# Layer 3's selective scan: the products du x B formed in PSUM by TensorE, tiles of two sequences by eight states, and every product with C on GpSimd

## The chip, the cores and the metric

The kernel runs on one core of a Trainium2 chip, in one launch. The metric is the device time of that core in microseconds (us), lower is better. The engines are called as the profile calls them: PE is TensorE (PEld its weight loads), DVE is VectorE, ACT is ScalarE, POOL is GpSimd, and SP is the engine whose queue issues the DMAs.

## The reference

The network has four layers in a row on an image batch of 8 x 64 x 64 x 64. Layers 0 to 2 (a spectral convolution and two state-space layers over whole images) are the same in both kernels. Layer 3 reads its input as one image of 64 channels by 128 by 128 and runs a bidirectional Mamba along one axis, and then another along the other. Cut to what matters, for one direction `i` of one axis:

```
xn = rms_norm(x, nw)
xc, z = split(xn @ ipw.T)                    # 256 channels each
xc = silu(causal_dwconv(xc, cw, cb))         # 4 taps
dt_, B, C = split(xc @ xpw.T)                # 4, 16 and 16 columns
dt = softplus(dt_ @ dtw.T + dtb)
h  = h * exp(dt[:, None] * A) + (dt * xc)[:, None] * B[None, :]     # a step of the scan, 256 x 16 states
y  = sum_n(h * C[None, :])
out = (y + D * xc) * silu(z) @ opw.T
```

The backward direction runs on the reversed sequence. Per axis the two outputs are joined, passed through a linear map and added to the input. The kernel takes sequences of 64 positions of its own layout; a scan must start anew at every sequence.

## The kernel before

`layer3` (from L1814) is a list of 256 steps: two axes `s`, sixteen chunks `c` of the image, four groups `g` of a chunk, and two directions `k`. A step holds eight sequences of 64 tokens, `W` = 512 tokens, for 256 channels. These lie as two halves `j` of 128 partitions beside each other, so that a tile is 128 x 1024 (`T` = 1024). `Step.prepare` makes a step's operands while the step before it is being scanned: the convolution as matmuls (L2004) and `u` by Silu (L2016), the projection (L2019), `dbl`, which is copied (L2022) and written to `bc` in HBM, `dt` (matmul L2028, Softplus at L415), `du` = dt x u (L2039, POOL), and `z` (L2042, L2052). At the first token of each sequence `dt` is set to 1e30 (L2056), so that the decay there is zero and one scan can run over all sequences.

`stream` (L433 on) runs over tiles, one for each of the 16 states `n` of each step, in an order written out by hand (`manual_schedule`). For each tile:

- `fetch` loads rows n of B and C, broadcast over the partitions, by one DMA (issued at L2060, 512 KB) into the pool `bc`;
- `multiply_b` (L484) forms hb = du x B on POOL, three tiles ahead;
- `decay` (L491) forms dA = exp(A dt) on ACT, in two halves;
- `scan` (L500) runs on DVE;
- `multiply_c` (L514) forms h x C, on POOL for the states in `Step.shared` (five of 16, or four in every fourth step) and on DVE for the others;
- `gather` sums the tile into `acc` in PSUM with the identity as weights (helper `mm`, L306: two matmuls of 128x512).

After 16 tiles `skip` (L2065) has added D x u, `drain` (L2069) multiplies acc with z, and after both directions `finish` makes the output (L2088, L2091, L2107). `begin` prepares the chunk to come: its input, the means of squares, their roots, and xn (L1967, POOL). The scratch tile `mm` in PSUM is one buffer that all preparation takes in turn. The tasks `begin` and `finish` advance by one piece at a time between tiles (`advance`).

Of the kernel before, what the change touches and what calls it, by code (L numbers as in the profile page):

```python
# [10 lines left out]
F32 = mybir.dt.float32  # L11
# [257 lines left out]
class Net:  # L269
# [1543 lines left out]

    def layer3(self, src, dst):  # L1814
# [8 lines left out]
        with ExitStack() as ctx:  # L1823
# [3 lines left out]
            pools = (pool("bc", 8), pool("hb", 4), pool("hc", 4), pool("h", 3), two(pool), pool("pa", 1, space=PSUM))  # L1827
            hp = pool("h3", 3, space=DRAM)

# [6 lines left out]
            class Weights:  # L1836
# [12 lines left out]
                def load(self):  # L1849
                    s = self.s  # L1850

                    spare = pools[0].tile([128, 2, W], F32, name="bc")
                    self.w_in = pools[0].tile([128, 2, W], F32, name="bc")
                    self.w_out = self.take("out", spare[:C, 0, :].rearrange("p (k t) -> p k t", k=2))
                    self.lin = spare[:C, 1, : 2 * C].rearrange("p (k t) -> p k t", k=2)
                    nc.sync.dma_start(self.lin, net.d["l3_lin"][:, s])
                    self.nw = self.take("nw")
                    self.take("in", self.w_in)


                    self.taps = [cp.tile([128, 2, 256], F32, name=f"taps{s}{k}") for k in range(2)]
                    for k in range(2):
                        for m in range(2):
                            for r in range(2):
                                row = net.d["l3_taps"][2 * s + k, m, r : r + 1, :]
                                nc.sync.dma_start(self.taps[k][r * C : r * C + C, m, :], row.to_broadcast([C, 256]))
                    self.cb, self.xp = self.take("cb"), self.take("xp")

                    both = cp.tile([128, 2, 256], F32, name=f"both{s}")
                    self.dtw, self.z = self.take("dtw", both[:4]), both[C:]  # L1870
                    self.dtb, self.A, self.D = self.take("dtb"), self.take("A"), self.take("D")

                def build(self):
                    s = self.s

                    ps = pools[5].tile([128, T], F32, name="acc")[:, : 4 * C]
# [41 lines left out]
            chunks = {}  # L1918

            def begin(s, c):  # L1920
# [35 lines left out]
                yield False  # L1956
                for r in range(2):
                    nc.sync.dma_start(
                        inv[r * C : r * C + C, :, ends[r]], row.rearrange("o (s t) -> o s t", t=HW).to_broadcast([C, 4 * H, HW])
                    )  # L1960
                yield False
                yield False
                yield False
                hold["xn"] = p2.tile([128, 4 * H, HW + 6], F32, name="xn")
                for g in range(4):
                    at = slice(g * H, g * H + H)
                    nc.gpsimd.tensor_tensor(hold["xn"][:, at], x[:, at], inv[:, at], ALU.mult)  # L1967

                    for _ in range(9 if g < 3 else 1):
                        yield False  # L1970
# [5 lines left out]
            class Step:  # L1976
                bc_shape, start, early, late = [128, 2, W], 1, 0, False
                first = staticmethod(lambda n: 0.0)
                keep = staticmethod(lambda n, h: None)
                shaped = staticmethod(lambda t: t.rearrange("p (j t) -> p j t", j=2))  # L1980
                spread = staticmethod(lambda t, m: t[:, m : m + 1, :].to_broadcast([128, 2, W]))

                def __init__(self, s, c, g, k):
                    self.s, self.c, self.g, self.k, self.rev = s, c, g, k, k == 1
                    self.w = weights[s]
                    self.shared = (2, 6, 10, 14) if k and g % 2 else (1, 4, 7, 10, 13)
                    self.lanes = [(slice(j * W, j * W + W), self.w.A[:, k, j, :]) for j in range(2)]
# [6 lines left out]
                def prepare(self):  # L1994
                    k, w, hold = self.k, self.w, chunks[self.s, self.c]
                    xn = hold["xn"][:, self.g * H : self.g * H + H, :]

                    def tokens(ps):
                        return ps.rearrange("p (s t) -> p s t", t=HW)

# [11 lines left out]
                    yield CALM  # L2012
                    u = self.u = p2.tile([128, T], F32, name="u")
                    for j in range(2):
                        at = slice(j * W, j * W + W)
                        nc.scalar.activation(u[:, at], px[:, at], AF.Silu, bias=w.cb[:, k, j : j + 1])  # L2016
                    pd = pp.tile([128, T], F32, name="mm")[:36, :W]
                    for j in range(2):
                        nc.tensor.matmul(pd, w.xp[:, k, j, :], u[:, j * W : j * W + W], start=j == 0, stop=j == 1)  # L2019
                    yield True  # L2020
                    dbl = p2.tile([36, W], F32, name="dbl")
                    nc.scalar.copy(dbl, pd)  # L2022
                    self.bc = hp.tile([NS, 2, W], F32, name="bc")
                    for m in range(2):
                        nc.sync.dma_start(self.bc[:, m, :], dbl[4 + m * NS : 4 + m * NS + NS])
                    pt = pp.tile([128, T], F32, name="mm")
                    for j in range(2):
                        nc.tensor.matmul(  # L2028
                            pt[:, j * W : j * W + W], w.dtw[:, k, j * 128 : j * 128 + 128], dbl[0:4], start=True, stop=True
                        )  # L2030
                    yield True
                    yield CALM
                    dt = self.dt = p2.tile([128, T], F32, name="dt")
# [4 lines left out]
                    du = self.du = p2.tile([128, T], F32, name="du")  # L2038
                    nc.gpsimd.tensor_tensor(du, dt, u, ALU.mult)  # L2039
                    pz = pp.tile([128, T], F32, name="mm")  # L2040
                    for j in range(2):
# [6 lines left out]
                        )  # L2048
                    yield True
                    yield CALM  # L2050
                    z = self.z = p2.tile([128, T], F32, name=f"z{k}")
                    nc.scalar.activation(z, pz, AF.Silu)  # L2052


                    at = HW - 1 if k else 0
                    nc.scalar.copy(dt.rearrange("p (s t) -> p s t", t=HW)[:, :, at], endless)  # L2056

                def load(self, n, t):
                    row = self.bc[n : n + 1].rearrange("o m t -> o (m t)")
                    nc.sync.dma_start(t.rearrange("p m t -> p (m t)"), row.to_broadcast([128, 2 * W]))  # L2060

                def skip(self, acc):
                    for j in range(2):
                        at = slice(j * W, j * W + W)
                        nc.tensor.matmul(acc[:, at], self.w.skip[self.k][:, j, :], self.u[:, at], start=True, stop=False)  # L2065
                    return True

                def drain(self, acc):
                    nc.vector.tensor_tensor(self.z, acc, self.z, ALU.mult)  # L2069
                    chunks[self.s, self.c][f"y{self.k}"] = self.z  # L2070

                def done(self):
# [4 lines left out]
                    if self.k == 0 and self.g == 0 and more < 4 * NB:  # L2077
# [34 lines left out]
            with tc.manual_schedule():  # L2112
# [10 lines left out]
                self.stream(pools, (6, 3, 6), steps, behind)  # L2123
# [26 lines left out]
```

## Time and profile before

| what | value |
| --- | --- |
| runs shown | 24,770.57, 24,780.73 and 24,781.64 us; median 24,780.73 |
| span of the profiled execution | 24,763.3 us, 17.4 us under that median (an own time of this execution is not given apart) |
| mean granted clock of TensorE | 0.940 |
| layer 3 in the span | from 11,517 us (first matmul of L2004) to the end, 13,246 us |
| a step of layer 3 (of 256) | 51.74 us |
| matmuls and weight loads in the span | 53,146 of each |

The page of a profile gives for each engine the busy time and its share of the span, then the span in 40 slices (each digit is the busy share in tenths, the row PEclk the granted clock). Groups of instructions are named by line, engine, operation and tiles, "out<-in", with shapes; after the bar come busy time and the mean duration of one in ns, and after the next bar the idle time of the engine before them with what ended it. A busy PE is not a PE at its peak: matmuls overlap, and their ends are modelled. A matmul of f32 operands appears in the trace as two MATMUL records with a weight load each.

### The profile page before, as it was taken

To read this page: it belongs to the slowest core of one execution; us is meant where nothing else is said; L and a number is where in the kernel's file an instruction comes from. 1 tells how busy PE (TensorE), PEld (TensorE's weight loads), DVE (VectorE), ACT (ScalarE), POOL (GpSimd) and SP (SyncE) were. 2 spreads that over 40 slices of the span, in tenths; PEclk is the share of its full clock that TensorE was granted. 3 is DMA by queue.
4 is the path that set the end of the run, shared out by engine and by line. 5 is a ranking of instruction groups with operands and counts; after the bars stand their busy time and mean duration, and the time that the engine had idled before them with its cause. 6 is when DMAs were issued, how large, how long until landed. Compare 5 with 4: busy or idle time off the path is not lost. (4 is left out here: it accounts for less than half of the span.)

```text
span 24763.3 us, 192937 instructions
## 1 busy us (share of the span) xinstructions
PE 21205.6 (86%) x53146; PEld 8272.3 (33%) x53146; DVE 22452.5 (91%) x12956; ACT 14796.2 (60%) x18824; POOL 22125.0 (89%) x10580
## 2 busy tenths in 40 slices
PE   8877888888888888888888888888888888888888
PEld 6522333333333323322333333333333333333333
DVE  5399999999999779978999999999999999999999
ACT  4355555555555456624666666666666666666666
POOL 0199999999999669977999999999999999999999
PEclk9888999999999999999999999999999999999999
DMA  2399899898998669933555555555555555555554
GB/s 65 93 319 326 308 321 318 310 319 314 313 318 311 238 211 339 343 103 93 168 173 169 173 167 173 168 173 167 173 169 173 168 173 169 173 169 173 169 173 158
DMA packets 1835292, 5282.68 MB, mean 213 GB/s; under 512 B 533712, under 2 KB 539924, under 8 KB 1831904
## 3 DMA queue, kind: packets, MB, share of 16 engines
q1 hardware_dynamic: 1809632, 5207.00, 63.0%
q10 hardware_dynamic: 24576, 63.33, 0.7%
q8 instruction: 423, 6.93, 0.1%
q14 instruction: 661, 5.41, 0.1%
HBM read 5112.85 MB, written 156.11 MB: 213 GB/s over the span
## 5 line engine op out<-in xcount | busy, mean ns | idle before, releaser
L484 POOL TENSOR_TENSOR hb<-du,bc 128x1024 f32<-128x1024 f32 x4608 | 10746.4, 2360 | 204.5 <-DVE h L500 137.9
L306 PE MATMUL acc<-hc,ident 128*128 128x512 f32 x18560 | 8788.0, 614 | 87.6 <-DVE img L1266 49.9
L491 ACT ACTIVATE dA<-dt,w_A 128x512 f32<-128x512 f32 x8192 | 5673.1, 693 | 3923.3 <-DVE hc L514 2873.1
L500 DVE TENSOR_TENSOR_SCAN dA<-dA,hb 128x1024 f32<-128x1024 f32 x3320 | 7580.9, 2283 | 188.4 <-ACT dA L491 101.0
L306 PE MATMUL acc<-h,ident 128*128 128x512 f32 x8064 | 4652.9, 706 | 2430.0 <-POOL h L514 2400.9
L306 PEld LDWEIGHTS acc<-hc,ident 128*128 128x128 f32 x18560 | 3639.8, 200 | 5214.2 <-issue 4562.5
L484 POOL TENSOR_TENSOR hb<-du,b 128x1024 f32<-128x1024 f32 x2048 | 4919.7, 2476 | 467.4 <-DVE dA L500 205.6
L514 DVE TENSOR_TENSOR hc<-dA,bc 128x1024 f32<-128x1024 f32 x3232 | 3956.8, 1224 | 244.4 <-issue 4.5
L491 ACT ACTIVATE dA<-dt,w_l_A 128x1024 f32<-128x1024 f32 x2560 | 2863.6, 1119 | 1004.6 <-DVE hc L514 764.6
L500 DVE TENSOR_TENSOR_SCAN h<-dA,hb 128x1024 f32<-128x1024 f32 x1416 | 3229.1, 2280 | 82.0 <-ACT dA L491 80.2
L306 PEld LDWEIGHTS acc<-h,ident 128*128 128x128 f32 x8064 | 1569.1, 212 | 5155.8 <-POOL h L514 3484.1
L514 POOL TENSOR_TENSOR h<-h,bc 128x1024 f32<-128x1024 f32 x1376 | 3243.1, 2357 | 8.3 <-DVE h L500 8.3
L500 DVE TENSOR_TENSOR_SCAN dA<-dA,carry,hb 128x1024 f32<-128x1024 f32 x1320 | 3094.2, 2344 | 124.9 <-POOL hb L484 57.2
L514 DVE TENSOR_TENSOR hc<-dA,c 128x1024 f32<-128x1024 f32 x1408 | 1723.7, 1224 | 118.3 <-DMA c<-bc 7.2
L514 POOL TENSOR_TENSOR h<-h,c 128x1024 f32<-128x1024 f32 x640 | 1566.4, 2447 | 7.5 <-ACT carry L1249 6.9
L491 ACT ACT_TABLE_LOAD x1128 | 1447.2, 1283 | 19.7
L500 DVE TENSOR_TENSOR_SCAN h<-dA,carry,hb 128x1024 f32<-128x1024 f32 x600 | 1404.6, 2341 | 36.4 <-ACT dA L491 25.2
L1249 ACT COPY carry<-dA 128x1 f32<-128x1 f32 x1056 | 169.4, 160 | 1654.3 <-DVE hc L514 1613.4
L2004 PE MATMUL mm<-xn,taps 128*128 128x512 f32 x2048 | 932.9, 597 | 1.1 <-ACT z L2052 1.1
L721 POOL MEMSET xf<- 128x24 f32 x33 | 4.3, 141 | 851.4 <-PE ps L742 725.2
L2019 PE MATMUL mm<-u,w_xp 128*36 128x512 f32 x1024 | 489.8, 601 | 143.0 <-ACT u L2016 136.3
L2039 POOL TENSOR_TENSOR du<-dt,u 128x1024 f32<-128x1024 f32 x256 | 603.0, 2355 | 9.9 <-ACT dt L415 9.9
(320 smaller groups left out, 18494.0 us busy)
## 6 DMA issues: line engine op xcount, KB each, us to landing
bc<-bc SPq DMA_DIRECT2D x4096, 512.0 KB
b<-bc SPq DMA_DIRECT2D x2048, 512.0 KB
c<-bc SPq DMA_DIRECT2D x2048, 512.0 KB
bc<-bc SPq DMA_DIRECT2D x512, 1024.0 KB
tmp<-rs SPq DMA_DIRECT2D x93, 512.0 KB
raw<-x SPq DMA_DIRECT2D x64, 512.0 KB
inv<-rs SPq DMA_DIRECT2D x64, 512.0 KB
tmp<-x SPq DMA_DIRECT2D x192, 128.0 KB
```

The source lines that it names most:

```text
L306: self.nc.tensor.matmul(o, lhsT, r, start=start, stop=stop)
L484: nc.gpsimd.tensor_tensor(s.shaped(hb[i]), s.shaped(s.du), B.pop(i), ALU.mult)
L491: nc.scalar.activation(dA[i][:, cut], s.dt[:, cut], AF.Exp, scale=A[:, n : n + 1])
L500: nc.vector.tensor_tensor_scan(h[:, way], dA[i][:, way], hb.pop(i)[:, way], s.first(n), ALU.mult, ALU.add)
L514: engine.tensor_tensor(s.shaped(o), s.shaped(h), CC.pop(i), ALU.mult)
L721: nc.gpsimd.memset(x[:, :, HW:], 0.0)
L1249: nc.scalar.copy(self.carry[:, n : n + 1], h[:, last : last + 1])
L2004: nc.tensor.matmul(tokens(px[:, j * W : j * W + W]), w.taps[k][:, m, j * 128 : j * 128 + 128], xn[:, :, f : f + HW], start=m == 0, stop=m ...
L2019: nc.tensor.matmul(pd, w.xp[:, k, j, :], u[:, j * W : j * W + W], start=j == 0, stop=j == 1)
L2039: nc.gpsimd.tensor_tensor(du, dt, u, ALU.mult)
```

## The change

Layer 3 runs a new function, `octets`, instead of `stream`. Layers 0 to 2 keep theirs.

A tile is still 128 x 1024 and there are still 16 for each step, but it now holds one half `j` of the channels, two sequences, eight states (half `q` of the 16) and 64 tokens. Four tiles (index `i` = 0 to 3, the eight sequences in pairs) make a group with one 128 x 4096 buffer `dA`; a step has four groups, (q, j) = (0,0), (0,1), (1,0), (1,1).

- *du x B.* In `prepare`, `du` is transposed by eight matmuls with the identity as moving operand and copied to `duT`, tokens on partitions; B is made a second time with tokens on partitions (eight matmuls with 16 columns) and copied to `BT`. `build` multiplies BT with a mask, so that `D` holds B on diagonals of 32 x 32 blocks, for eight states beside each other (DVE, 128x1024, twice a step). `spread` then makes a tile of hb directly in PSUM by four matmuls, each with 32 rows of duT as weights and 256 columns of D. Tokens lie in halves of 32 (`h`); `e` is the sequence of the pair. hb has two buffers of two banks, sequence e in bank e.
- *Scan* (DVE) reads dA and hb from PSUM, and writes in place over dA.
- *Products with C* (`multiply`) are all on POOL, in place. The row of C is loaded for one (q, i) and used for both j: eight DMAs of 512 KB for a step; B is no longer broadcast by DMA.
- *gather* sums a group, when its four tiles are multiplied, by eight matmuls of 128x512 with the identity, four in each of two iterations.
- xn is formed for one step of two (k = 0) in `prepare` instead of ahead for a whole chunk, and `begin` waits with its broadcast of `inv` until the chunk before has formed all its xn.

In every iteration t the order of issue is: the DMA for t+4, the product with C of tile t-1, the matmuls of hb for t+1, the exps of the next group (3, 3, 2 and 0 of the eight), the sums (where t mod 4 is 1 or 2), the scan of t, the drain, and a piece of preparation.

The diff, cut to its core:

```diff
+    def octets(self, pools, steps, behind):
...
+        def where(t):
+            s, r = divmod(t, per)
+            q, j = first.supers[r // 4]
+            return steps[s], q, j, r % 4
...
+        def fetch(t):
+            if t < total:
+                s, q, j, i = where(t)
+                if j == 0:
+                    need(t, "bc")
+                    tile_ = cp_.tile([128, T], F32, name="c")
+                    nc.sync.dma_start(tile_, s.row(q, i).to_broadcast([128, T]))
+                    for e in range(first.lanes):
+                        CC[t + 4 * e] = tile_
+        def decay(g, ns):
+            if 4 * g < total:
+                need(4 * g, "dt")
+                s, q, j, _ = where(4 * g)
+                if ns[0] == 0:
+                    sup[g] = sp.tile([128, 8, 8, 64], F32, name="dA")
+                for n in ns:
+                    o = sup[g][:, :, n, :].rearrange("p s (h t) -> p s h t", h=2)
+                    nc.scalar.activation(o, s.times(j), AF.Exp, scale=s.rates(j)[:, 8 * q + n : 8 * q + n + 1])
+        def spread(t):
+            if t < total:
+                need(t, "duT")
+                s, q, j, i = where(t)
+                o = hb[t] = hbp[t % 2].tile([128, 2, 8, 64], F32, name="hb")
+                Q, g0 = divmod(2 * i, 4)
+                for h in range(2):
+                    for e in range(2):
+                        at = slice(32 * (g0 + e), 32 * (g0 + e) + 32)
+                        nc.tensor.matmul(
+                            o[:, e, :, 32 * h : 32 * h + 32],
+                            s.duT[at, j, 2 * h + Q, :],
+                            s.D[q][at, 2 * h + Q].rearrange("p n t -> p (n t)"),
+                            start=True,
+                            stop=True,
+                        )
+        def part(t):
+            i = t % 4
+            return sup[t // 4][:, 2 * i : 2 * i + 2].rearrange("p s n t -> p (s n t)")
+        def scan(t):
+            s = steps[t // per]
+            way = slice(None, None, -1) if s.rev else slice(None)
+            h, x = part(t), hb.pop(t).rearrange("p s n t -> p (s n t)")
+            nc.vector.tensor_tensor_scan(h[:, way], h[:, way], x[:, way], 0.0, ALU.mult, ALU.add)
+        def multiply(t):
+            nc.gpsimd.tensor_tensor(part(t), part(t), CC.pop(t), ALU.mult)
+        def gather(g, ns):
+            s, q, j, _ = where(4 * g)
+            if ns[0] == 0 and q == 0:
+                acc[j] = pa.tile([128, 512], F32, name="acc")
+                s.skip(j, acc[j])
+            o = acc[j].rearrange("p (s t) -> p s t", t=64)
+            for n in ns:
+                nc.tensor.matmul(o, self.ident, sup[g][:, :, n, :], start=False, stop=q == 1 and n == 7)
+            if ns[-1] == 7:
+                sup.pop(g)
+        work, self.held, self.urgent = Task(steps[0].prepare()), None, deque()
+        work.run()
+        for q in range(2):
+            steps[0].build(q)
+        for t in range(4):
+            fetch(t)
+        decay(0, range(8))
+        spread(0)
+        work = None
+        for t in range(total + 4):
+            at, r = divmod(t, per)
+            more = at + 1 < len(steps)
+            if r == 0 and more:
+                steps[at + 1].ready()
+                while self.held or self.urgent:
+                    self.advance(behind)
+                work = Task(steps[at + 1].prepare())
+            fetch(t + 4)
+            if 0 < t <= total:
+                multiply(t - 1)
+            if r == 2 and 0 < at < len(steps):
+                steps[at].build(1)
+            if r == per - 5 and more:
+                need(t + 5, "duT")
+                steps[at + 1].build(0)
+            spread(t + 1)
+            ns = (range(3), range(3, 6), range(6, 8), ())[t % 4]
+            if ns:
+                decay(t // 4 + 1, ns)
+            if t >= 5 and t % 4 in (1, 2):
+                g = (t - 5) // 4
+                if 4 * g < total:
+                    gather(g, range(4) if t % 4 == 1 else range(4, 8))
+            if t < total:
+                scan(t)
+            if t >= 7 and t % 4 == 3:
+                s, q, j, _ = where(t - 7)
+                if q == 1:
+                    s.drain(j, acc.pop(j))
+                    if j == first.lanes - 1:
+                        s.done()
+            if work is not None and not (self.held and work.said is None):
+                work.step()
+                if work.over:
+                    work = None
+            self.advance(behind, work is None or work.said is not True)
+        while behind or self.urgent or self.held:
+            self.advance(behind)
...
-            pools = (pool("bc", 8), pool("hb", 4), pool("hc", 4), pool("h", 3), two(pool), pool("pa", 1, space=PSUM))
+            hbp = [pool(f"hb{j}", 1, space=PSUM) for j in range(2)]
+            pools = (pool("dA", 3), pool("cc", 6), pool("D", 2), hbp, pool("pa", 2, space=PSUM))
             hp = pool("h3", 3, space=DRAM)
+            mask = cp.tile([128, 32], F32, name="mask")
+            nc.vector.tensor_tensor(mask, self.ident[:, :32], self.ident[:, 32:64], ALU.add)
+            for r in range(2, 4):
+                nc.vector.tensor_tensor(mask, mask, self.ident[:, 32 * r : 32 * r + 32], ALU.add)
...
+                while c and used.get((s, c - 1), 0) < 4 or s and not c and used.get((0, 2 * NB - 1), 0) < 4:
+                    yield False
...
-                yield False
-                yield False
-                hold["xn"] = p2.tile([128, 4 * H, HW + 6], F32, name="xn")
-                for g in range(4):
-                    at = slice(g * H, g * H + H)
-                    nc.gpsimd.tensor_tensor(hold["xn"][:, at], x[:, at], inv[:, at], ALU.mult)
-                    for _ in range(9 if g < 3 else 1):
-                        yield False
...
+                lanes, supers = 2, [(0, 0), (0, 1), (1, 0), (1, 1)]
                     self.s, self.c, self.g, self.k, self.rev = s, c, g, k, k == 1
-                    self.w = weights[s]
-                    self.shared = (2, 6, 10, 14) if k and g % 2 else (1, 4, 7, 10, 13)
-                    self.lanes = [(slice(j * W, j * W + W), self.w.A[:, k, j, :]) for j in range(2)]
+                    self.w, self.D = weights[s], {}
...
-                    xn = hold["xn"][:, self.g * H : self.g * H + H, :]
+                    at = slice(self.g * H, self.g * H + H)
+                    if k == 0:
+                        xn = hold["xn"] = p2.tile([128, H, HW + 6], F32, name="xn")
+                        nc.gpsimd.tensor_tensor(xn, hold["x"][:, at], inv[:, at], ALU.mult)
+                        used[self.s, self.c] = self.g + 1
+                        yield
+                    xn = hold["xn"]
...
-                        nc.scalar.activation(u[:, at], px[:, at], AF.Silu, bias=w.cb[:, k, j : j + 1])
-                    pd = pp.tile([128, T], F32, name="mm")[:36, :W]
+                        o, x = halves(u[:, at]), px[:, at].rearrange("p (s h t) -> p s h t", h=2, t=32)
+                        nc.scalar.activation(o, x, AF.Silu, bias=w.cb[:, k, j : j + 1])
+                    yield
+                    pd = pp.tile([128, T], F32, name="mm")
                     for j in range(2):
-                        nc.tensor.matmul(pd, w.xp[:, k, j, :], u[:, j * W : j * W + W], start=j == 0, stop=j == 1)
-                    yield True
-                    dbl = p2.tile([36, W], F32, name="dbl")
-                    nc.scalar.copy(dbl, pd)
-                    self.bc = hp.tile([NS, 2, W], F32, name="bc")
-                    for m in range(2):
-                        nc.sync.dma_start(self.bc[:, m, :], dbl[4 + m * NS : 4 + m * NS + NS])
+                        o = pd[:36, :W].rearrange("p (s h t) -> p s h t", h=2, t=32)
+                        nc.tensor.matmul(o, w.xp[:, k, j, :], halves(u[:, j * W : j * W + W]), start=j == 0, stop=j == 1)
+                    for m in range(4):
+                        for j in range(2):
+                            nc.tensor.matmul(
+                                pd[:, W + m * NS : W + m * NS + NS], chunk(u, j, m), w.xp[:, k, j, 4 : 4 + NS], start=j == 0, stop=j == 1
+                            )
+                    yield True
+                    dbl = p1.tile([36, W], F32, name="dbl")
+                    nc.scalar.copy(dbl, pd[:36, :W])
+                    BT = self.BT = p2.tile([128, 4, NS], F32, name="BT")
+                    nc.scalar.copy(BT.rearrange("p m n -> p (m n)"), pd[:, W : W + 4 * NS])
+                    bc = hp.tile([2, 8, 8, HW], F32, name="bc")
+                    for q in range(2):
+                        at = 4 + NS + 8 * q
+                        nc.sync.dma_start(bc[q].rearrange("s n t -> n s t"), dbl[at : at + 8].rearrange("n (s t) -> n s t", t=HW))
+                    self.bc = bc
+                    yield
                     pt = pp.tile([128, T], F32, name="mm")
                     for j in range(2):
-                        nc.tensor.matmul(
-                            pt[:, j * W : j * W + W], w.dtw[:, k, j * 128 : j * 128 + 128], dbl[0:4], start=True, stop=True
-                        )
-                    yield True
-                    yield CALM
-                    dt = self.dt = p2.tile([128, T], F32, name="dt")
+                        o = pt[:, j * W : j * W + W].rearrange("p (h s t) -> p h s t", h=2, t=32)
+                        x = dbl[0:4].rearrange("p (s h t) -> p h s t", h=2, t=32)
+                        nc.tensor.matmul(o, w.dtw[:, k, j * 128 : j * 128 + 128], x, start=True, stop=True)
+                    yield True
...
-                    du = self.du = p2.tile([128, T], F32, name="du")
-                    nc.gpsimd.tensor_tensor(du, dt, u, ALU.mult)
...
+                    du = p1.tile([128, T], F32, name="du")
+                    nc.gpsimd.tensor_tensor(du, dt, u, ALU.mult)
+                    yield True
                     z = self.z = p2.tile([128, T], F32, name=f"z{k}")
                     nc.scalar.activation(z, pz, AF.Silu)
-                    at = HW - 1 if k else 0
-                    nc.scalar.copy(dt.rearrange("p (s t) -> p s t", t=HW)[:, :, at], endless)
-                def load(self, n, t):
-                    row = self.bc[n : n + 1].rearrange("o m t -> o (m t)")
-                    nc.sync.dma_start(t.rearrange("p m t -> p (m t)"), row.to_broadcast([128, 2 * W]))
-                def skip(self, acc):
+                    at = (1, 31) if k else (0, 0)
                     for j in range(2):
-                        at = slice(j * W, j * W + W)
-                        nc.tensor.matmul(acc[:, at], self.w.skip[self.k][:, j, :], self.u[:, at], start=True, stop=False)
-                    return True
-                def drain(self, acc):
-                    nc.vector.tensor_tensor(self.z, acc, self.z, ALU.mult)
+                        o = dt[:, j * W : j * W + W].rearrange("p (h s t) -> p h s t", h=2, t=32)[:, at[0], :, at[1]]
+                        nc.scalar.copy(o, endless[:, :8])
+                    self.dt = dt
+                    yield
+                    pu = pp.tile([128, T], F32, name="mm")
+                    for j in range(2):
+                        for m in range(4):
+                            at = (j * 4 + m) * 128
+                            nc.tensor.matmul(pu[:, at : at + 128], chunk(du, j, m), net.ident, start=True, stop=True)
+                    yield True
+                    duT = p2.tile([128, 2, 4, 128], F32, name="duT")
+                    nc.scalar.copy(duT.rearrange("p j m d -> p (j m d)"), pu)
+                    self.duT = duT
+                def build(self, q):
+                    o = self.D[q] = pools[2].tile([128, 4, 8, 32], F32, name="D")
+                    nc.vector.tensor_tensor(
+                        o,
+                        mask.unsqueeze(1).unsqueeze(1).to_broadcast([128, 4, 8, 32]),
+                        self.BT[:, :, 8 * q : 8 * q + 8].unsqueeze(3).to_broadcast([128, 4, 8, 32]),
+                        ALU.mult,
+                    )
+                def times(self, j):
+                    return self.dt[:, j * W : j * W + W].rearrange("p (h s t) -> p s h t", h=2, t=32)
+                def rates(self, j):
+                    return self.w.A[:, self.k, j, :]
+                def row(self, q, i):
+                    return self.bc[q].rearrange("s n t -> (s n t)").unsqueeze(0)[:, i * T : i * T + T]
+                def skip(self, j, acc):
+                    u = self.u[:, j * W : j * W + W].rearrange("p (h s t) -> p s h t", h=2, t=32)
+                    acc = acc.rearrange("p (s h t) -> p s h t", h=2, t=32)
+                    nc.tensor.matmul(acc, self.w.skip[self.k][:, j, :], u, start=True, stop=False)
+                def drain(self, j, acc):
+                    z = self.z[:, j * W : j * W + W]
+                    nc.vector.tensor_tensor(z, acc, z, ALU.mult)
                     chunks[self.s, self.c][f"y{self.k}"] = self.z
...
-                    if self.k == 0 and self.g == 0 and more < 4 * NB:
+                    if self.k == 0 and self.g == 1 and more < 4 * NB:
...
-                self.stream(pools, (6, 3, 6), steps, behind)
+                self.octets(pools, steps, behind)
```

## The prediction

> **What bounds the kernel now.** I read the shares and slices of the page first, then busy time by stretch, then the groups of layer 3, then the timeline. Layer 3 runs from its first convolution matmul (L2004) at 11,517 us to the end of the span: 13,246 us for 256 steps, **51.74 us a step**. On the page:
>
> ```profile
> PE 21205.6 (86%) x53146; PEld 8272.3 (33%) x53146; DVE 22452.5 (91%) x12956; ACT 14796.2 (60%) x18824; POOL 22125.0 (89%) x10580
> PE   8877888888888888888888888888888888888888
> DVE  5399999999999779978999999999999999999999
> POOL 0199999999999669977999999999999999999999
> PEclk9888999999999999999999999999999999999999
> ```
>
> Layers 0 to 2 are not touched, so only the right half matters. There DVE and POOL are full, and PE is less full, though by little. A stretch inside layer 3 puts figures on it:
>
> ```profile
> core 0: us, PE busy (x) PEld busy (x) DVE busy (x) ACT busy (x) POOL busy (x), PEclk, DMA share, GB/s
> 16000.00:20000.00 4000.00, 3468.72 (x7287) 1319.14 (x7288) 3881.15 (x2199) 2722.73 (x3587) 3946.67 (x1724) 0.95 0.53 171
> ```
>
> POOL is busy 98.7% (51.1 us a step), DVE 97.0% (50.2), PE 86.7% (44.9), ACT 68.1% (35.2). POOL and DVE bound the stage together. The groups of layer 3 (12,000 to 24,000 us) give the prices:
>
> ```profile
> L484 POOL TENSOR_TENSOR hb<-du,bc 128x1024 f32<-128x1024 f32 x3720 | 8673.1, 2360 | 153.7 <-DVE h L500 118.3 <-DVE dA L500 34.9
> L500 DVE TENSOR_TENSOR_SCAN dA<-dA,hb 128x1024 f32<-128x1024 f32 x2616 | 5972.1, 2283 | 13.7 <-ACT dA L491 8.4 <-POOL hb L484 5.0
> L306 PE MATMUL acc<-hc,ident 128*128 128x512 f32 x10462 | 4912.4, 613 | 0.0
> L514 DVE TENSOR_TENSOR hc<-dA,bc 128x1024 f32<-128x1024 f32 x2615 | 3201.6, 1224 | 198.5 <-issue 4.0 <-PE acc L306 0.9 <-PE mm L2019 0.4
> L514 POOL TENSOR_TENSOR h<-h,bc 128x1024 f32<-128x1024 f32 x1105 | 2604.6, 2357 | 0.0
> ```
>
> The reader is to see that a product with B or C costs 2.36 us on POOL and 1.22 us on DVE, and a scan 2.28 us. The matmul's 613 ns is no price: matmuls overlap. The timeline has it:
>
> ```profile
> 20035.49 1.98 PE L306 MATMUL acc<-h,ident 128*128 128x512 f32 x4 [0.59 <-POOL h L514]
> 20037.40 1.98 PE L2042 MATMUL mm<-xn,both 64*128 64x512 f32 x4
> 20039.32 3.70 PE L306 MATMUL acc<-hc,ident 128*128 128x512 f32 x8
> ```
>
> Each f32 matmul is recorded as two passes; at full clock a 512-column pass starts every 0.429 us, so a 128x512 matmul holds PE for **0.86 us**. Between 20037.40 and 20039.32 lie 1.92 us for four passes (1.72): going to another shape of the array (64 rows here) costs **0.20 us**, of which 0.09 is the change and 0.10 a first weight load that nothing hides.
>
> [...] the 4-row matmuls of L2028 also start 0.429 us apart. [...] Layer 0 shows such pairs, 48 rows in each of two row groups:
>
> ```profile
> 639.72 2.00 PE L692 MATMUL pw<-w_l_phi,w_l_theta 48*128 48x256 f32 x16 [0.46 <-DVE W L299]
> ```
>
> Sixteen passes of 256 columns in 2.00 us, the last 0.16 of it pipeline tail: eight slots of 0.216 plus 0.10 at the start. Alone they would need 16 x 0.214 = 3.4. So two-way overlap is real, each matmul with weights of its own. [...] A scan from PSUM is not in the trace; the nearest row, z<-acc (L2069), takes 1.21 us from PSUM beside 1.22 for the SBUF product.
>
> **The change, part by part, per step.**
> *POOL.* Sixteen products du x B go (16 x 2.36 = -37.8). All products with C come to POOL: 16 x 2.36 instead of 4.75 on average. With du (2.36) and half of an xn (1.40) it has 37.8 + 2.4 + 0.7 = **40.8 us**.
> *DVE.* Loses 11.25 products (x 1.224 = -13.8), gains two builds of the diagonal blocks (128x1024, 2 x 1.22). Scans 36.5 + builds 2.4 + drains 1.3 = **40.3**.
> *ACT.* The exps keep number and size. Added: a copy of BT and one of duT (1.03, as z<-mm). About **37**.
> *DMA.* Eight rows of C of 512 KB instead of sixteen of B and C: the queue's load halves. It bounds nothing now (share 0.53), and the rows are asked for four tiles ahead, over 12 us, so I count no gain and no loss.
> *PE* gets what POOL loses:
> - sums into acc, 32 matmuls as before: 64 x 0.429 = 27.5
> - preparation as before: passes of 512 columns for taps 8, xp 4, dtw 4, z 4, skip 4, the output 5 (ten every second step), the mean 1: 30 x 0.429 = 12.9. (27.5 + 12.9 = 40.4 is today's sum; with the clock at 0.95 and tails it shows as 44.9.)
> - du x B: each tile has four matmuls of 32 rows and 256 columns, eight passes. Neighbours in the order lie in different row groups [...], so I take pairs: 4 slots x 0.216 = 0.86; 16 tiles: **13.8**. Bounds: 6.9 if four ran at once (but the third and fourth use the same row groups as the first two), 27.6 if none overlap.
> - eight small matmuls for BT and eight transposes of du, 32 passes. The nearest row, pt<-x of layer 0 with 128 columns, starts a pass every 0.11 us: 3.4.
> - changes of shape: per four tiles one burst, half a sum, a burst, half a sum, two bursts: four changes x 0.20, sixteen a step, and about nine around preparation and output: 5.0.
>
> Sum **62.6 us**, beside 40.8 on POOL: PE becomes the bound.
>
> *The new wait.* hb has two buffers, and the burst for tile t+1 waits for scan t-1; everything in PE's queue, the sum after it included, waits behind. Per four tiles by these durations: burst 0 to 1.0, half sum to 4.6, burst to 5.7, half sum to 9.2, two bursts to 11.3. The scan of the third burst runs from 10.5 to 12.8, and the next burst waits for it: 1.6 us idle in every 12.9. Preparation that falls there hides it (about two and a half of four times), leaving about **2.4 us**. What sat before scans and sums until now (hb from POOL, h from POOL, hc from DVE) goes, because these engines have over 20 us of slack.
>
> So 62.6 + 2.4 = **65.0 us a step**: (65.0 - 51.74) x 256 = +3,395 us. Added to the profiled span of 24,763.3 that is 28,158; the median of the runs is 17.4 us above the span, so **28,175 us**.
>
> **The rivals.**
> 1. *Pairs don't overlap with 32 rows* (shown only for 48 and 64). Burst 1.73: +13.8 a step, 78.8, so 31,700. Against it: layer 0 overlaps at the same 256 columns with weights loaded for each. 8%.
> 2. *The scan from PSUM is dearer.* It decides from about 3.8 us (16 x 3.8 + 3.8 = 64.6 on DVE); doubled to 4.56 it gives 16 x 4.56 + 3.8 = 77, about 31,200. Against it: z<-acc. Were it quicker than 2.28, only the 2.4 us of wait could go. 5%.
> 3. *The clock.* It stands at 0.95 [...]; but if thin bursts counted as idle, each tenth of PE's time at half clock adds 6.3 us a step, 1,600 us: 29,800. 4%.
> 4. *Other side: faster.* If the bursts ran nearly free beside other matmuls, POOL at 40.8 would set the pace, about 44 with its waits: (44 - 51.74) x 256 = -1,980, so 22,800. It decides only where PE falls below 51.7, that is where a burst costs under 0.2 us instead of 1.0 with its part of waits and changes. Even four at once (0.43) leaves 65.0 - 6.9 = 58. Against it: the sums fill all 128 rows. 2%, and 1% for no change.
>
> The order is written out by hand, so no scheduler can leave a product elsewhere; that the change doesn't do what it says I don't count.
>
> **How the numbers follow.** PE-bound with pairs has 80%. Its own ends: 61.1 us (wait filled, part of the changes hidden) gives 27,150; 71.3 (each wait for a scan open, PE held by ACT in preparation) gives 29,800, which takes in the mild case of the clock. The range 27,150 to 29,800 leaves out the rest. A measurement tells about 0.2%, 50 us, from no change; all main cases lie far beyond: slower 97%, same 1%, faster 2%.
>
> **What would show it.** Right: in layer 3 PE near 95% or more and PEclk near 1.0, DVE and POOL near 63%; PE idle mostly before L1869 and released by DVE scans; eight L1869 passes in about 1.0 us; shares of L1897 as those of L306 now. Wrong: eight passes in 1.7 us or more (rival 1), scans over 3 us (rival 2), PEclk under 0.9 (rival 3), or POOL near full with PE waiting for it.

## The result and the profile after

The changed kernel takes **28,495.5 us** (28,483.8 to 28,510.1), the kernel before 24,775.7 on the same chip: ratio **1.150, 95% interval 1.149 to 1.152**. The forecast was 28,175 us, in a range of 27,150 to 29,800. Layer 3 starts at 11,516 us as before (11,517) and ends the span at 28,488.7: 16,973 us, **66.3 us a step** instead of 51.74. The forecast was 65.0.

Shares and slices of the page, after:

```profile
PE 25730.0 (90%) x94106; PEld 11526.8 (40%) x94106; DVE 19878.4 (70%) x10847; ACT 14667.3 (51%) x19623; POOL 19925.3 (70%) x9364
PE   8778888888888889899999999999999999999999
DVE  5499999999986997566666666666666656666655
POOL 0399999999984996566666666666666666666666
PEclk9889999999999999899999999999999999999999
```

In the right part DVE and POOL have gone from 9 to 6, and PE from 8 to 9. The stretch inside layer 3, after (busy time of each engine, then granted clock, DMA share, GB/s):

```profile
16000.00:20000.00 4000.00, 3774.27 (x15350) 1796.40 (x15349) 2420.59 (x1217) 2101.36 (x2991) 2559.55 (x1059) 0.94 0.23 69
```

PE is busy 94.4%, DVE 60.5%, POOL 64.0%, and the DMA share has fallen from 0.53 to 0.23; it bounded nothing before, so that gains nothing. The groups of layer 3, after (12,000 to 28,000 us):

```profile
L1888 POOL TENSOR_TENSOR dA<-dA,c 128x1024 f32<-128x1024 f32 x3871 | 9525.4, 2473 | 5575.5 <-DVE dA L1885 5560.1
L1885 DVE TENSOR_TENSOR_SCAN dA<-dA,hb 128x1024 f32<-128x1024 f32 x3871 | 8724.1, 2278 | 5669.8 <-PE hb L1869 5117.6 <-PE mm L2184 494.3 <-POOL dA L1888 57.9
L1897 PE MATMUL acc<-dA,ident 128*128 128x512 f32 x15485 | 7662.6, 641 | 0.0
L1869 PE MATMUL hb<-D,duT 32*128 32x256 f32 x30968 | 3628.0, 411 | 817.2 <-DVE dA L1885 817.2
```

Read the idle columns as a chain: POOL waits for the scan, the scan waits for hb from PE, and PE alone waits little (817 us, for scans that free an hb buffer). The scan from PSUM costs 2.278 us, no more than the one from SBUF (2.283). The timeline of one stretch, after, PE's lines alone:

```profile
20003.06 1.13 PE L1869 MATMUL hb<-D,duT 32*128 32x256 f32 x8
...
20007.76 1.16 PE L1869 MATMUL hb<-D,duT 32*128 32x256 f32 x16
...
20058.01 1.16 PE L1869 MATMUL hb<-D,duT 32*128 32x256 f32 x16
...
20061.63 1.13 PE L1869 MATMUL hb<-D,duT 32*128 32x256 f32 x8 [2.46 <-DVE dA L1885]
...
20062.69 5.40 PE L1897 MATMUL acc<-dA,ident 128*128 128x512 f32 x8
```

Three things are in it. A burst (the four matmuls, eight passes, that make one tile of hb) takes 1.06 us to the next start when it stands alone, as forecast. **Two bursts on end (x16) that start together take no longer than one** (1.16 us against 1.13): four row groups at once. And after the wait of 2.46 us the eight passes of the sum take 5.40 us instead of 3.70, because part of them runs at half clock.

From the same trace, for each step: PE idle 3.7 us (5.6% of 66.3), of which 3.4 are waits for scans; by the clock's own record 7.4 us at half clock (between 12,000 and 24,000 us in 182 stretches of 3.41 us, 67 of 6.83 and 23 of 10.24), with PE busy in 7.2 of them, where it does half the work (a pass of 512 columns starts every 0.85 us there instead of 0.43): 3.6 us lost; what is left, 66.3 - 3.7 - 3.6 = **59.0 us, is PE's work at full clock**. All experiments below are read by this sum of three terms.

### The profile page after: what moved, and what is told of

It is laid out like the page before. It is cut to its first block, busy times and chain, and to the rows that moved or that the text cites. A ratio compares the mean times of both kernels' runs of the same rounds, so it can differ in the third digit from the quotient of the medians.

```text
span 28488.7 us, 260989 instructions
## 1 busy us (share of the span) xinstructions
PE 25730.0 (90%) x94106; PEld 11526.8 (40%) x94106; DVE 19878.4 (70%) x10847; ACT 14667.3 (51%) x19623; POOL 19925.3 (70%) x9364
## 4 chain that ended last, share of the span: by engine, by line
PE 58%; DVE 3%; ACT 1%; issue 0%; POOL 0%; DMA 0%; SPq 0%; POOLq 0%; ACTq 0%; DVEq 0%
PE acc L1897 28%; PE hb L1869 12%; PE mm L2146 3%; DVE dA L1885 3%; PE acc L2242 2%; PE mm L2268 2%; PE mm L2166 2%; PE mm L2163 2%; PE mm L2215 2%; PE mm L2193 2%; PE mm L2184 1%; PE pc L376 1%; PE mm L306 1%; PE ps L376 1%; PE mm L2265 0%
## 5 line engine op out<-in xcount | busy, mean ns | idle before, releaser
L1888 POOL TENSOR_TENSOR dA<-dA,c 128x1024 f32<-128x1024 f32 x4096 | 10076.6, 2472 | 5914.8 <-DVE dA L1885 5898.6
L1885 DVE TENSOR_TENSOR_SCAN dA<-dA,hb 128x1024 f32<-128x1024 f32 x4096 | 9230.8, 2278 | 6012.2 <-PE hb L1869 5415.4
L1897 PE MATMUL acc<-dA,ident 128*128 128x512 f32 x16384 | 8115.2, 641 | 1.2 <-POOL dA L1888 1.2
L1897 PEld LDWEIGHTS acc<-dA,ident 128*128 128x128 f32 x16384 | 3217.6, 204 | 4249.5 <-issue 4247.5
L1869 PE MATMUL hb<-D,duT 32*128 32x256 f32 x32768 | 3842.6, 411 | 880.1 <-DVE dA L1885 879.0
L1869 PEld LDWEIGHTS hb<-D,duT 32*128 32x128 f32 x32768 | 2379.6, 188 | 2743.4 <-issue 1371.7
L306 PE MATMUL acc<-hc,ident 128*128 128x512 f32 x7040 | 3370.8, 616 | 89.6 <-DVE img L1266 48.4
L306 PE MATMUL acc<-h,ident 128*128 128x512 f32 x3200 | 1868.2, 714 | 869.5 <-POOL h L514 841.8
L306 PEld LDWEIGHTS acc<-hc,ident 128*128 128x128 f32 x7040 | 1390.0, 201 | 2082.3 <-issue 1705.4
L484 POOL TENSOR_TENSOR hb<-du,bc 128x1024 f32<-128x1024 f32 x512 | 1196.3, 2357 | 33.6 <-DMA bc<-bc 21.9
L500 DVE TENSOR_TENSOR_SCAN dA<-dA,hb 128x1024 f32<-128x1024 f32 x440 | 1006.0, 2286 | 155.4 <-ACT dA L491 78.2
```

Of the source, the lines that this page charges most:

```text
L306: self.nc.tensor.matmul(o, lhsT, r, start=start, stop=stop)
L484: nc.gpsimd.tensor_tensor(s.shaped(hb[i]), s.shaped(s.du), B.pop(i), ALU.mult)
L500: nc.vector.tensor_tensor_scan(h[:, way], dA[i][:, way], hb.pop(i)[:, way], s.first(n), ALU.mult, ALU.add)
L1869: nc.tensor.matmul(o[:, e, :, 32 * h : 32 * h + 32], s.duT[at, j, 2 * h + Q, :], s.D[q][at, 2 * h + Q].rearrange("p n t -> p (n t)"), star ...
L1885: nc.vector.tensor_tensor_scan(h[:, way], h[:, way], x[:, way], 0.0, ALU.mult, ALU.add)
L1888: nc.gpsimd.tensor_tensor(part(t), part(t), CC.pop(t), ALU.mult)
```

## The experiments

The theory: PE's work, plus its waits for scans, sets the step. Rivals: the bursts' overlap or PE's work is incidental, and the loop of burst and scan sets the step (B); the products with C, all on POOL, hold up the sums (C). Ratios below are to the kernel before, timed on the same chip; differences in us are to the changed kernel's 28,495.

**POOL's load halved.**

```diff
 def multiply(t):
-    nc.gpsimd.tensor_tensor(part(t), part(t), CC.pop(t), ALU.mult)
+    c = CC.pop(t)
+    if t % 2:
+        nc.gpsimd.tensor_tensor(part(t), part(t), c, ALU.mult)
```

> POOL leaves out the product with C for every second tile (so half of the products are missing from the result); nothing else changes. Theory A: POOL has 23 us of slack a step, so the time stays within 0.5% of 28,490 us. Rival C (all products with C on one engine are the bottleneck through the sums that wait for them): POOL's 40 us a step fall by 19 us and the time falls by several per cent, to 27,500 us or less.

Measured: 28,477.9 us, ratio 1.150 (1.149 to 1.152), no change. The stretch in this kernel:

```profile
16000.00:20000.00 4000.00, 3774.35 (x15353) 1796.42 (x15350) 2409.04 (x1217) 2101.93 (x2991) 1361.82 (x574) 0.94 0.22 70
```

POOL's busy time (fifth engine column) falls from 2,560 to 1,362 us and nothing else moves. Rival C is out: fewer products on POOL gain nothing.

**Half of the sums.**

```diff
 for n in ns:
-    nc.tensor.matmul(o, self.ident, sup[g][:, :, n, :], start=False, stop=q == 1 and n == 7)
+    if n % 2:
+        nc.tensor.matmul(o, self.ident, sup[g][:, :, n, :], start=False, stop=q == 1 and n == 7)
```

> gather sums only every second state (16 of the 32 matmuls of 128x512 a step are left out, so y lacks half of its terms). Theory A: PE loses 16 x 0.86 = 13.7 us a step, and the wait for the scan may take back up to 3 us of it: 51.5 to 55.5 us a step, 24,700 to 25,750 us. Rival B (the loop of burst and scan sets the step): the loop holds 4 scans of 2.28 us in a group, so little changes: over 27,400 us.

Measured: 25,307.1 us, ratio 1.022 (1.020 to 1.023): 53.95 a step, 12.4 less. The terms: idle 2.8, lost to half clock 4.8, work 46.4. Work fell by 12.6 (59.0 to 46.4), near the 13.7 counted; the clock took 1.2 of it back, and idle time gave 0.9. Rival B is out, and the price of a sum matmul is right within a tenth. The stretch in this kernel:

```profile
16000.00:20000.00 4000.00, 3790.16 (x16489) 1846.04 (x16489) 3031.26 (x1497) 2567.86 (x3669) 3142.65 (x1302) 0.91 0.28 86
```

**The order within a burst.**

```diff
-for h in range(2):
-    for e in range(2):
+for e in range(2):
+    for h in range(2):
```

> The loops over h and e in spread change places, so that neighbouring matmuls of a burst use the same 32 rows; the same four matmuls, the same columns. Theory A (PE sets the step, and its bursts run in pairs of row groups): only the second and third matmul of a burst still differ in rows, so a burst holds PE for three matmuls of 0.43 us instead of two: +0.43 x 16 = +6.9 us a step, about 30,260 us, +6%. Rival B (the pairs give nothing, or the step is set by the loop burst - scan - burst and PE's share of it is incidental): within 1% of the changed kernel.

Measured: 28,535.3 us, ratio 1.153 (1.151 to 1.154). Not the 30,260 of theory A. The timeline of this kernel says why:

```profile
20000.54 1.14 PE L1869 MATMUL hb<-D,duT 32*128 32x256 f32 x8
20001.61 3.70 PE L1897 MATMUL acc<-dA,ident 128*128 128x512 f32 x8
20005.24 1.17 PE L1869 MATMUL hb<-D,duT 32*128 32x256 f32 x16
```

A burst still takes 1.07 us, and its passes start in pairs (13 ns apart, instead of 6). So exchanging the order within a burst did not undo the pairs. The run could not tell theory from rival B; what it disproved is my picture, in which only neighbours pair. The next one takes the second row group away.

**One row group.**

```diff
-at = slice(32 * (g0 + e), 32 * (g0 + e) + 32)
+at = slice(32 * g0, 32 * g0 + 32)
```

> Both sequences of a burst read the same 32 rows of duT and D (the values of the second sequence are those of the first, so the result is not the reference's); columns, weights and number of matmuls stay. Theory A', after the trace of the run with h and e exchanged (its bursts still show pairs 13 ns apart): [...] it is the second row group that halves a burst. Then a burst alone holds PE for 4 x 0.43 = 1.73 us instead of 0.86, two bursts on end 1.73 instead of 0.9, three 2.6 instead of 1.7: per step 5.9 x 0.86 + 2.5 x 0.85 + 1.4 x 0.9 + 0.9 = +9.3 us, of which the waits may take back up to 2: 30,300 to 30,900 us. Rival B (bursts don't matter): within 1% of 28,490 us.

Measured: 33,413.8 us, ratio 1.348 (1.346 to 1.350): 85.4 a step, far above the range expected. The terms: idle 2.1, lost to half clock 12.1, work 71.3. Work rose by 12.3 where 9.3 were expected, and a burst alone now takes 1.92 us from start to start: +0.86, exactly the second row group. So the overlap is real and worth some 12 us a step. What was not foreseen is that bursts on end no longer overlap much: two take 2.9 us to the next start (1.36 on average in the changed kernel), and in all 351 such pairs between 12,000 and 24,000 us the second burst starts only with the fifth of the first one's eight passes. The clock, of which I had expected nothing, cost another 8.5; the stretch shows it at 0.86:

```profile
16000.00:20000.00 4000.00, 3900.85 (x11921) 2094.08 (x11920) 1888.36 (x945) 1620.94 (x2312) 1986.94 (x823) 0.86 0.17 54
```

**The sums respread.**

```diff
-if t >= 5 and t % 4 in (1, 2):
+if t >= 5 and t % 4 in (1, 3):
```

> The second half of each group's sums moves from the iteration with t mod 4 = 2 to that with t mod 4 = 3, so that no two bursts stand behind a burst whose scan has not begun. Work and result are the same. Theory A with the wait as forecast: the wait of PE for scans (3.7 us a step in the changed kernel) goes nearly to nothing: -3 to -3.7 us a step, about 27,600 us. If the stretches at half clock (11% of layer 3) come from that wait, they go too: up to 3 us more, 26,800 us. Rival (the wait is hidden by preparation anyway, and PE's own work sets everything): within 0.5% of 28,490 us.

Measured: 27,264.0 us, ratio 1.101 (1.099 to 1.103): 4.3% faster than the changed kernel with the same work. The terms: idle 1.35 (from 3.7), lost to half clock 2.3 (from 3.6), work 57.8 (from 59.0; 5.6 pairs of bursts stand on end in a step instead of 2.5 pairs and 1.4 threes, which may be why). The wait is where the forecast put it, and not hidden. What is left of it is one wait of 2.0 us in every second step, in iteration 1 of a backward step. The stretch:

```profile
16000.00:20000.00 4000.00, 3911.73 (x16547) 1880.08 (x16546) 2595.03 (x1313) 2254.14 (x3216) 2761.81 (x1142) 0.96 0.24 75
```

**All sums at once.**

```diff
-if t >= 5 and t % 4 in (1, 2):
+if t >= 5 and t % 4 == 1:
...
-    gather(g, range(4) if t % 4 == 1 else range(4, 8))
+    gather(g, range(8))
```

> All eight sums of a group stand in the iteration with t mod 4 = 1 instead of four and four. Work and result are the same; eight changes of the array's shape a step fall away (8 x 0.20 = -1.6 us), but by the hand-worked schedule of the forecast a group takes 14.1 us instead of 12.9 before preparation fills its gaps. Theory A: the wait outweighs the changes, +1 to +4 us a step, 28,750 to 29,500 us. Rival (changes of shape are the dear part): below 28,490 us.

Measured: 30,543.0 us, ratio 1.234 (1.232 to 1.236). The stretch:

```profile
16000.00:20000.00 4000.00, 3621.59 (x13689) 1759.69 (x13687) 2174.54 (x1086) 1860.19 (x2656) 2278.27 (x944) 0.87 0.20 62
```

The direction is right and the size is not: 74.3 a step, 8.0 more where 1 to 4 were expected. Idle is 7.0 (+3.3), lost to half clock 9.4 (+5.8, which was not in the sum), and work 57.9 (-1.1, near the 1.6 counted for the changes of shape that fall away). So this order costs more through the clock than through idle time.

**The wait filled.** This was to tell whether idle time causes the half clock. In two places extra matmuls go ahead of a burst. It is not the burst that waits, but the one before it: the fill must stand behind the burst whose scan is awaited, and ahead of the burst that waits.

```diff
 Q, g0 = divmod(2 * i, 4)
+r = (t - 1) % per
+if t and (r == 12 or r == 0 and s.k == 1):
+    for e in range(2):
+        fill = s.duT.rearrange("p j m d -> p (j m d)")[:, :512]
+        nc.tensor.matmul(o[:, e].rearrange("p s t -> p (s t)"), self.ident, fill, start=True, stop=True)
```

> In the two places of a pair of steps... where PE waits for a scan and no preparation falls there (iteration 12 of every step, and iteration 0 before a forward step), two extra matmuls of 128x512 are put ahead of the burst, 1.72 us of full-array work whose result the burst overwrites. Theory D (the idle stretch of 2.5 us is what takes the clock to half for the next 3.4 to 6.8 us, 3.6 us lost a step): the extra work fits into the idle time, the clock rises to 0.97 or more in layer 3, and the time FALLS by 1 to 2.5 us a step, 27,850 to 28,250 us. Rival E (the clock falls for the thin bursts or for another reason): the clock stays at 0.94, and the time stays within 0.4% of 28,490 or rises.

Measured: 27,957.4 us, ratio 1.129 (1.127 to 1.130). **More work for PE made the kernel 538 us faster**, 2.1 us a step. In the stretch PE is busy 99.7% and the clock is 0.98:

```profile
16000.00:20000.00 4000.00, 3986.43 (x16230) 1911.94 (x16229) 2501.99 (x1256) 2164.61 (x3083) 2646.58 (x1094) 0.98 0.23 72
```

Idle fell from 3.7 to 0.2 and the loss to half clock from 3.6 to 1.2, against 3.8 more work. Without the wait, two thirds of the clock's loss are gone.

**The wait filled with thin work.** The same two places, with the burst itself three times instead of the extra matmuls:

```diff
+r = (t - 1) % per
+for _ in range(3 if t and (r == 12 or r == 0 and s.k == 1) else 1):
     for h in range(2):
         for e in range(2):
```

> In the same two places as in the run with the extra full-array matmuls, the burst itself is repeated twice more instead (1.73 us of 32-row matmuls, the same values written again). The result is the same. Theory D (an idle PE takes the clock down): as there, the idle time is filled, the clock rises to 0.96 or more, about 27,960 us. Theory D' (what takes the clock down is a stretch with little of the array in use, and bursts of 32 rows count as nearly idle): the clock stays at 0.94 or falls, and the time stays at 28,490 us or rises by up to 1.5%.

Measured: 27,922.2 us, ratio 1.128 (1.126 to 1.130); clock 0.98 in the stretch:

```profile
16000.00:20000.00 4000.00, 3923.27 (x17362) 1942.84 (x17361) 2503.31 (x1259) 2165.92 (x3083) 2648.11 (x1094) 0.98 0.23 71
```

Idle is 1.2 a step here, lost to half clock 1.2. The time is the one forecast by theory D (27,960), and D' falls as it was put: with bursts in two groups of 32 rows in place of the wait the clock rose as far as with full matmuls. That idle time alone takes the clock down doesn't follow: the run of one row group, with only 2.1 us idle, stayed at 0.86.

**Respread and filled.** One extra matmul in the respread kernel at `(t - 1) % 8 == 6`.

> The respread sums, and one extra 128x512 matmul ahead of the burst in iterations 6 and 14 of each step, where that kernel's trace still has PE idle (1.35 us a step). Theory D and D': the idle time is filled and part of the 2.3 us lost to half clock comes back: 60 to 61 us a step, 26,880 to 27,140 us. If the clock there falls for the bursts of 32 rows, the same as the respread sums alone, 27,264 us, or up to 1% more.

Measured: 27,697.4 us, ratio 1.119 (1.117 to 1.120): 433 us slower than the respread sums alone, neither of the two expected values. Idle stayed at 1.35 and the half clock nearly so (2.0 lost): the fill stood in iterations 6 and 14, the wait of that kernel is in iteration 1, and so the fill was simply work. It cost 1.8 us a step. In these two runs a fill paid (538 us) between the burst whose scan is awaited and the burst that waits for it, and cost 433 us elsewhere.

**States folded on DVE.** On top of the respread sums DVE adds four of the eight states to the other four, and PE sums the rest:

```diff
+def fold(g, late):
+    a = sup[g][:, 4 * late : 4 * late + 4]
+    nc.vector.tensor_tensor(a[:, :, :4], a[:, :, :4], a[:, :, 4:], ALU.add)
...
-if t >= 5 and t % 4 in (1, 3):
-    g = (t - 5) // 4
...
-        gather(g, range(4) if t % 4 == 1 else range(4, 8))
+if t >= 6 and t % 4 in (2, 3):
+    g = (t - 6) // 4
...
+        gather(g, range(2) if t % 4 == 2 else range(2, 4))
...
 scan(t)
+if t >= 3 and t % 4 in (3, 1) and (t - 3) // 4 * 4 < total:
+    fold((t - 3) // 4, t % 4 == 1)
```

> On top of the respread sums, DVE adds states 4 to 7 of a group to states 0 to 3 (two additions of 1024 elements a group, 8 x 1.22 = 9.8 us a step), and gather sums four states instead of eight (16 matmuls of 0.86 us less, -13.7 us on PE). Work and result are the same. Theory A: PE's work falls to 57.7 - 13.7 = 44 us, DVE rises to 36.5 + 2.8 + 1.4 + 9.8 = 50.5 and becomes the bound; with waits 52 to 55 us a step, 24,850 to 25,600 us. Rival B (PE's work is not what counts): above 26,500 us.

Measured: 27,442.9 us, ratio 1.108 (1.106 to 1.110). A miss: 62.1 a step, not 52 to 55.

```profile
16000.00:20000.00 4000.00, 3601.97 (x14289) 1750.25 (x14286) 3320.48 (x1811) 2233.61 (x3184) 3143.51 (x1127) 0.85 0.24 74
```

PE's work did fall, to 47.1 us, but idle grew to 6.2 and the loss to half clock to 8.8; DVE is busy 83% and bounds nothing either. The likely reading, which no run isolates, is that three engines with some 50 us each and two hb buffers between them wait for each other in turn. The instructions also got dearer beside each other: a product with C takes 2.82 us instead of 2.48 in the respread kernel, a build 2.28 instead of 1.44. The next run, with the builds on POOL too (`nc.gpsimd.tensor_tensor` in `build`):

> The former, and the builds of the diagonal blocks move from DVE to POOL (2.8 us off DVE, about 4.7 onto POOL). DVE 47.7, POOL 47.4, PE 44 us a step: the three stand level. Theory A: 50 to 54 us a step, 24,300 to 25,350 us; if the builds delay the products with C that the sums wait for, the upper end or the same as the former.

Measured: 27,400.4 us, ratio 1.106 (1.104 to 1.108), 0.2% less than the former. Levelling the load in this way brings next to nothing. No version here beats the kernel before; the best of the new order that does all the work is the respread one, 10% slower than before.

## Why the prediction was right, and where its sum was off

The mechanism stands step by step. PE became the bound: halving POOL's products changes nothing, halving PE's sums takes 12.4 us off a step. The new wait is PE's burst waiting for a scan, and moving the sums removes most of it. The scan from PSUM is no dearer (2.278), so rival 2 is out; matmuls in two row groups overlap with 32 rows (0.97 us from a burst's first start to the end of its last slot, and +0.86 without the second row group), so rival 1 is out; POOL and DVE at 64% and 60% leave the faster side nothing.

The total, 65.0 forecast and 66.3 measured, is closer than its terms:

| term, us a step | forecast | measured |
| --- | --- | --- |
| bursts | 13.8 | about 11.7 |
| everything else on PE at full clock | 48.8 | about 47.3 (59.0 less the bursts) |
| idle | 2.4 | 3.7 (3.4 of it waiting for scans) |
| lost to half clock | 0 | 3.6 |
| step | 65.0 | 66.3 |

- *Bursts* were mis-sized. I let four matmuls run together nowhere, since those of one burst share two row groups. But bursts on end lie in different groups: a step has 5.9 bursts alone (0.86 each), 2.5 twos (1.16 on average: 0.9 where both start together, more where the second comes later), 1.4 threes (2.0 without their wait), and one in two halves beside L2184 (0.9 together): 5.1 + 2.9 + 2.8 + 0.9 = 11.7, by the starts in the trace, the changes of shape left out. The bound "6.9 if four ran at once" was stated, and the value taken lay too high.
- *The wait* was right in cause and place and too small. My schedule gave 1.6 us idle a group before preparation; the open ones, 1.4 a step where 1.5 were forecast, measure 2.46 at most. This error has the same root as the first: from the start of two bursts on end to the next burst the forecast had 3.6 us, and the trace has 3.62 (20058.01 to 20061.63). The scans took what was forecast; the two bursts took 1.1 us instead of 2.1, and PE waited longer. The other 0.3 us of idle time stand before the means of squares and were not in the sum.
- *The clock* was missed. I named a PEclk near 1.0 as a sign of being right; it stayed at 0.94 (0.95 before), with PE busy 94.4% instead of 86.7%. The sum put it at nothing, although the kernel before already lost 2.2 us a step (5.2 us at half clock). Most of the waits of 2.46 us are followed by a stretch at half clock (203 of 249 between 12,000 and 24,000 us within 5 us), and filling them takes two thirds of the loss away (3.6 to 1.2). Rival 3 named the clock and blamed thin bursts. It was half right at most: with bursts in two row groups in place of the wait the clock was 0.98, with all bursts in one row group 0.86.

So errors of -2.1, -1.5, +1.3 and +3.6 us left +1.3: that the total is closer than its terms is luck.

## What to carry to other kernels

Before work is moved onto the engine with slack, count that engine's passes in the stage: here 11 us of slack (PE with 40.4 us of work in 51.7) were to hold 22 us of new work by the forecast's own sum. In a loop with two buffers, place the long work of the bound engine so that a consumer has started before its next buffer is asked for; one digit in a condition was worth 4.3%. When TensorE is the bound, price what its waits do to the clock as well: the changed kernel lost 3.6 us a step beside 3.7 idle, the one with all sums at once 9.4 beside 7.0. In the kernel before, with 7.0 us idle and 2.2 lost a step, it went by the length of the waits: between 12,000 and 24,000 us none of 469 waits of 0.3 to 1.8 us was followed by half clock within 5 us, 74 of 195 from 1.8 to 3.2 us were, and all 146 of more than 3.2 us. The length alone doesn't tell it in the changed kernel: there the clock fell in or within 5 us after all 46 waits of 1.0 and 1.7 us too, beside 203 of the 249 of 2.46.

## What the runs showed of the hardware that I had not expected

- Exchanging the loops left the passes of a burst in pairs (13 ns apart, 1.07 us a burst; 28,535 us against 28,495), where I had expected 6.9 us more a step. Bursts on end ran in four row groups at once (sixteen passes of 256 columns in 1.16 us, eight in 1.13); with one row group in a burst two of them took 2.9 us to the next start instead of 1.36. What decides which matmuls run together was not shown.
- Extra matmuls can pay: 538 us less with two more in each of the two places, clock 0.98 instead of 0.94 in the stretch.
- With one group of 32 rows in a burst, 24.9 us of an 85.4 us step ran at half clock although PE was idle for 2.1 us only; in the changed kernel, with two groups, it was 7.4 us of 66.3 with 3.7 idle. Two groups in place of the wait gave a clock of 0.98, the same as full matmuls there. So in these runs idle time alone doesn't give the time at half clock; that the rows in use count beside it is my reading, and by how much was not shown.
